# The time-step projection of a decoder block: four token sections side by side on four column groups of the matrix engine

## The chip, the cores and the metric

The kernel runs on one core of a Trainium2 chip. The time of a run is device time in microseconds; the kernel before was run three times (1519.18, 1522.98 and 1523.01 us), and its time is the median, 1522.98 us. One more execution was taken with the hardware profiler on. Profile and trace come from that one.

The engines that matter here: PE multiplies matrices (PEld is its loading of the stationary operand, which overlaps PE), DVE, ACT and POOL work on vectors, and SP only issues DMAs, in order. ACT issues some DMAs as well. DMAs of both run on the same 16 DMA engines.

## The reference

The reference is one decoder block for a batch of two sequences of 2048 tokens with 512 features: a Mamba-2 state-space mixer, a cross-attention over 77 context tokens, and a mixture of 16 expert slots, each added to its input and normalised. The change touches only the beginning of the mixer, the time step and its decay:

```python
proj = xs @ W_in.T
xBC, dt = (proj[..., :d_conv_c], proj[..., d_conv_c:])
...
dt = jax.nn.softplus(dt + dt_bias)
...
A = A_param * dt
cumA = jnp.cumsum(A, axis=1)
norm = (jnp.exp(cumA) * jnp.cumsum(jnp.exp(-cumA), axis=1))[..., None]
Y = ssd(xh, A, Bh, Ch, CHUNK)
out = Y[0] / norm
```

So for each token and each of 16 heads there is one number `dt`, the product of the token's 512 features with one column of `W_in`; it is summed along all 2048 tokens. Only the output of the scan of batch 0 is used (`Y[0]`), while the normaliser `norm` is taken of both batches.

## The kernel before

The work comes in stages. The first (lines 297 to 675, up to about 325 us of the span) has the in-projection, the convolution and the scan over 16 chunks of 128 tokens, for batch 0 alone, and beside them `decay` for batch 0 and for batch 1. The second mixes the tokens up to the second norm (up to about 950 us), then come the experts' weights, read from memory, and the combination of the slots.

`decay(b)` (line 373) works on a tile `z` of 128 rows by 512 columns. Its rows are four sections of 512 tokens, 32 rows each, of which 16 hold the heads; its columns are the tokens of a section. For each section `g` a tile `xs` with the section's tokens is loaded from `xT` (features on partitions, in four blocks `k` of 128) and multiplied with `wdt`, the 32 columns of the weight (16 of them zero), so that the result lands in the 32 rows of section `g` of a PSUM tile `dps`. For batch 0 `xs` holds all 512 tokens of a section (1 MB, in the buffers named "CS"); for batch 1 it holds 256 (512 KB, in the buffers named "sw"). Both have two buffers, which they share with others: "CS" with the scan's operand `CS` and one of the first weights, "sw" with the weights that `setup` loads. Then DVE adds the bias and copies the section's 32 rows to `z` (line 385), and the generator yields. After four sections, `decay` goes on with all of `z`: softplus, the sums along the tokens (`full_scan`, line 361), the weights `wtok` that the scan of batch 0 needs, and the normalisers `fd`, stored for the next stage.

All matmuls go through the helper `mm` (line 231 in the profile), copies through `cp` (line 234), the division of a number into a high and a low part through `split` (lines 234 and 242). The matmuls of `decay` are in float32, and such a matmul leaves two records in the trace; those of the projection, `pj`, are products of such high and low parts.

The order of the work is written down: `project`, `scan`, `decay`, `setup` and others are generators, and strings such as the one for the opening, `'PPPFFPPFPFPPPDDPPPPPDPPPPDDPPPPPSSSDSPSSSSS'`, say which of them takes the next step. D is a step of `decay(0)`; in the later strings V is one of `decay(1)`, U one of `setup`, S one of the scan and P one of the projection. A scheduler of the framework then orders the instructions of each engine's queue from that, by a simulation of its own. Each queue runs in its order.

In the first stage SP issues the loads of `xs`, the first weights, the stores of the projection's high and low parts (line 540), the loads of the scan's operands BS and CS from there (line 554, six for each chunk), the loads of `setup` (line 417), and the store of `fd` (line 410). The tokens for the projection (`xt`, line 321) are loaded by ACT's queue.

Of the kernel before, what the change touches and what calls it, by code (L numbers as in the profile page):

```python
# [8 lines left out]
FP = mybir.dt.float32  # L9
FR = mybir.dt.float32r  # L10
AF = mybir.ActivationFunctionType
ALU = mybir.AluOpType
# [13 lines left out]
# columns of the packed per-partition vectors  # L26
# [3 lines left out]
# columns of the packed shape constants  # L30
# [34 lines left out]
def merge(*flows):  # L65
    """Emit flows side by side, each given as (generator, steps), at the pace that ends them together."""
    todo = [[f, n, 0] for f, n in flows]
    while todo:
        f = min(todo, key=lambda t: t[2] / t[1])
        f[2] += 1  # L70
        try:
            next(f[0])
        except StopIteration:
            todo.remove(f)


def weave(flows, depth, lag):
    """Emit `depth` flows side by side; the next one starts `lag` steps after the last."""
# [145 lines left out]
def tile_decoder(ctx, tc, a, out, dbg=None, upto=9, opt=None):  # L224
# [68 lines left out]
    with ExitStack() as st:  # L293
        class Pools:
            """tiles by tag from pools of their own, so that the next phase takes over each pool's room as it falls free"""
# [33 lines left out]
        def first_operands():  # L329
            """the first tokens and the weights in the order of their use, in pieces"""  # L330
# [22 lines left out]
        # decay: dt, cumulative sums, normalisers in rows (section of 512 tokens, head)  # L353
# [19 lines left out]
        def decay(b):  # L373
            z, za, cum = (sb.tile([128, 512], FP, tag="dec", bufs=3, name=n) for n in ("z", "za", "cum"))
            for g in range(4):
                dps = ps.tile([128, 512], FP, tag="p", bufs=3, name="dps")
                gs = slice(32 * g, 32 * g + 32)
                w = 256 if b else 512
                for t in range(0, 512, w):
                    xs = sb.tile([128, 4, w], FP, tag="sw" if b else "CS", bufs=2, name="xs")  # L380
                    (nc.sync, nc.scalar)[EA.get("dq%d" % b, 0)].dma_start(
                        xs, a["xT"][b][:, g * 512 + t:g * 512 + t + w].rearrange("(k p) t -> p k t", p=128))
                    for k in range(4):
                        mm(dps[gs, t:t + w], wdt[:, k, :], xs[:, k, :], k == 0, k == 3)
                dve.tensor_scalar(z[gs, :], dps[gs, :], vec[gs, V_DTB:V_DTB + 1], None, ALU.add)
                yield
# [26 lines left out]
        def setup():  # L413
            """operands of the next phase from weights, a half at a time"""
# [5 lines left out]
            # cross-attention keys and values  # L420
# [32 lines left out]
            # dispatch queries folded with the key weights  # L453
# [91 lines left out]
        def scan_loads(c):  # L545
            """operands of one pass that holds the three hi/lo products of the 32 state rows"""
# [13 lines left out]
        def scan_ready(c):  # L560
            """token-major x (weighted) and B of a chunk"""
# [79 lines left out]
        def next_weights():  # L641
            """weights of the next phase, into the room that the in-projection's leave"""
# [8 lines left out]
        def spread(*flows):  # L651
            """names side by side, each given as (name, steps), at the pace that ends them together"""
            return "".join(n for _, _, n in sorted(((k + 1) / n, i, c) for i, (c, n) in enumerate(flows) for k in range(n)))
# [30 lines left out]
    def stats(pool_, z, p=128, tg=""):  # L684
        """mean and 1/std over the free axis of z [p, 512]; the latter from exp(-ln(var+eps)/2) and a Newton step"""
# [13 lines left out]
    with ExitStack() as st:  # L699
# [222 lines left out]
        # Two half periods of four quarters for every tile; a stage works on the tile `back` periods ago.  # L922
        # Each quarter holds one group of heads of the attention and one block of products.
# [5 lines left out]
        def period(p):  # L929
            """operations of one period, in the order of their issue"""  # L930
# [86 lines left out]
    if True:  # L1017
# [17 lines left out]
        # the combine's weights stay in the slabs 0, 1, 2: the keys' come before the last experts', the others after  # L1035
# [34 lines left out]
        # sums over the tokens, divided by the sums of the weights, with their features on the partitions  # L1070
# [20 lines left out]
        # the slots after the dispatch and their norm; feature 4p+j sits on partition p  # L1091
# [17 lines left out]
        def mean(v):  # L1109
            """mean over the features, on all partitions"""  # L1110
# [33 lines left out]
    if True:  # L1144
# [4 lines left out]
        def beat(e, at):  # L1149
            """scores of the tokens in the waits for the last expert's weights"""  # L1150
# [105 lines left out]
        # what the slots hold besides the experts' sums  # L1256
# [8 lines left out]
        def slots_now(on):  # L1265
            """the slots with what the experts gave so far"""
# [8 lines left out]
        def slot_heads(nm, on, PS, pool_, tags=("kr0", "kr1")):  # L1275
            """keys or values of the slots without their bias, features on the partitions"""
# [11 lines left out]
        def by_heads(dst, src, cv, n):  # L1288
            """block-diagonal over the heads of a group"""
# [25 lines left out]
        def early():  # L1315
            """the scores of all slots but the last experts': maxima, exponentials and their sums"""
# [44 lines left out]
    with ExitStack() as st:  # L1361
# [18 lines left out]
        def slot_outputs(b, m):  # L1380
            """values of the slots times the output weights for two groups of heads"""
# [4 lines left out]
        def split_outputs(b, m):  # L1386
            vp = vps.pop((b, m))
            if m == 0:
                # the weights of a head sum to one, so that its rows carry the output bias
# [203 lines left out]
```

## Time and profile before

| what | value |
|---|---|
| median of three runs | 1522.98 us |
| the runs | 1519.18 to 1523.01 us |
| span of the profiled execution, the only time given of it | 1526.7 us |
| PE busy | 1372.1 us, 90% |
| DVE busy | 905.6 us, 59% |
| ACT busy | 616.3 us, 40% |
| POOL busy | 446.2 us, 29% |
| `dps` matmuls | 96 records, 24.2 to 197.9 us |
| loads of `xs` | 12 DMAs, landing 4.1 to 10.9 us after issue |

A line of the chain of waits has a start, a length and what ran; "PE dps L231 x8" means eight records of matmuls that write `dps`. A line of the busy time by stretch has the stretch, its length, the busy time of PE, PEld, DVE, ACT and POOL, each with its number of instructions, then the granted clock of PE as a share of full speed, the share of time that the DMA engines were busy, and the GB/s that they moved. A row of a DMA view gives packets and bytes; a packet is one contiguous run. In a line of the waits, the engine and line on the left waited for what stands right of the arrow; then come the sum in us, the number of waits and the longest. Matmuls overlap, and the end of each is modelled, so a "busy" PE can hide short gaps.

### The profile page before, as it was taken

The numbers are of one execution on the slowest core, as the hardware profiler recorded it, in microseconds if no ns is written. First come the engines' busy times: TensorE is split into PE (matmuls) and PEld (weight loads), VectorE is DVE, ScalarE is ACT, GpSimd is POOL, SyncE is SP. The second block draws the span as 40 slices with busy tenths as digits, with TensorE's granted clock in tenths as the row PEclk, the third lists the DMA queues.
The fourth block names the chain that finished last, engine by engine and source line by source line (L and its number), as shares of the span: only waits on it lengthen the run. The fifth ranks groups of instructions, "written<-read, shape, count | busy, mean of one in ns | idle before, by whom it ended". The sixth has DMA issues, their size and how long they took to land.

```text
span 1526.7 us, 27382 instructions
## 1 busy us (share of the span) xinstructions
PE 1372.1 (90%) x10282; PEld 996.3 (65%) x10282; DVE 905.6 (59%) x2142; ACT 616.3 (40%) x1683; POOL 446.2 (29%) x496
## 2 busy tenths in 40 slices
PE   7899999978999999999999997948979788889896
PEld 5788889857888888888888875205544445433364
DVE  6897796856788888888888764001211111115597
ACT  5544443524565565665656552001000000104456
POOL 3644543535444444444443321000000000000054
PEclk9999998988999999999999998969989998999998
DMA  9797987895122221311110138898999999999447
GB/s 312 194 214 206 227 219 194 223 248 143 56 56 60 66 63 57 96 57 56 57 53 18 70 139 350 355 415 359 418 419 418 420 419 419 418 421 408 174 149 251
DMA packets 177499, 339.61 MB, mean 222 GB/s; under 512 B 12027, under 2 KB 123131, under 8 KB 152536
## 3 DMA queue, kind: packets, MB, share of 16 engines
q1 hardware_dynamic: 161072, 311.25, 58.5%
q10 hardware_dynamic: 16296, 26.62, 5.1%
q8 instruction: 81, 1.33, 0.4%
q14 instruction: 50, 0.41, 0.1%
HBM read 299.56 MB, written 38.27 MB: 221 GB/s over the span
## 4 chain that ended last, share of the span: by engine, by line
PE 60%; DVE 17%; DMA 15%; ACT 4%; issue 3%; SPq 1%; POOL 1%; ACTq 0%; POOLq 0%; DVEq 0%
PE mm L231 25%; DMA ew<-in_e_W 8%; PE pj L231 7%; PE up L231 7%; DMA ew<-in_e_Wg 5%; PE tr L826 3%; PE yac L231 2%; PE sc L231 2%; PE y L231 2%; PE dps L231 2%; PE uu L231 2%; PE gp L231 1%; DVE X L528 1%; ACT pp L816 1%; PE tr L719 1%
## 5 line engine op out<-in xcount | busy, mean ns | idle before, releaser
L231 PE MATMUL up<-ew,hT 128*32 128x512 f32 x944 | 134.7, 645 | 34.4 <-DMA ew<-in_e_W 30.9
L818 POOL TENSOR_TENSOR pp<-pp,den 128x308 f32<-128x308 f32 x128 | 90.1, 708 | 161.4 <-DVE den L817 109.0
L1174 ACT ACTIVATE sv<-up 128x512 f32<-128x512 f32 x32 | 19.1, 597 | 269.8 <-PE up L231 247.0
L1183 POOL MEMSET aT<- 128x512 f32 x16 | 8.3, 524 | 403.5 <-PE yac L231 401.8
L231 PE MATMUL mm<-xTh,cqh 128*128 128x256 f32 x256 | 76.2, 309 | 26.2 <-ACT xTh L234 26.2
L1233 DVE TENSOR_TENSOR Qc<-mm,vec 128x512 f32<-128x512 f32 x32 | 22.1, 691 | 125.3 <-PE mm L231 125.3
L242 DVE TENSOR_TENSOR xTl<-tr,xTh 128x512 fp32r<-128x512 f32 x32 | 21.3, 687 | 115.1 <-ACT xTh L234 115.0
L231 PEld LDWEIGHTS up<-ew,hT 128*32 128x32 f32 x944 | 26.0, 112 | 96.6 <-issue 56.7
L826 PE MATMUL tr<-cst,pp 128*77 128x128 f32 x512 | 80.6, 282 | 1.4 <-ACT pt L234 1.2
L231 PE MATMUL mm<-x1Th,w30h 128*128 128x256 f32 x256 | 76.9, 301 | 4.4 <-DVE ql L786 3.6
L816 ACT ACTIVATE pp<-sc,mx 128x77 f32<-128x77 f32 x240 | 75.4, 327 | 13.3 <-DVE mx L813 12.5
L234 ACT COPY pt<-tr 77x512 f32<-77x512 f32 x96 | 55.7, 582 | 61.2 <-PE tr L826 34.2
L231 PE MATMUL mm<-xTl,cqh 128*128 128x256 f32 x256 | 78.4, 308 | 1.2 <-DVE xTl L242 1.2
L231 PEld LDWEIGHTS mm<-xTh,cqh 128*128 128x128 f32 x256 | 51.5, 207 | 40.2 <-ACT xTh L234 30.2
L231 PE MATMUL mm<-xTh,cql 128*128 128x256 f32 x256 | 75.2, 296 | 0.0
L231 PE MATMUL mm<-x1Tl,w30h 128*128 128x256 f32 x256 | 74.4, 291 | 0.9 <-DVE x1Tl L722 0.9
L231 PE MATMUL mm<-x1Th,w30l 128*128 128x256 f32 x256 | 73.8, 288 | 0.0
L826 PEld LDWEIGHTS tr<-cst,pp 128*77 128x77 f32 x512 | 59.4, 148 | 16.3 <-issue 11.1
L234 ACT COPY raw<-pj 128x512 f32<-128x512 f32 x48 | 28.1, 584 | 99.1 <-PE pj L231 65.0
L231 PE MATMUL yac<-ew,aT 128*32 128x512 f32 x488 | 61.1, 637 | 7.1 <-issue 4.7
L744 POOL TENSOR_TENSOR ut<-ut,fb 128x512 f32<-128x512 f32 x32 | 41.0, 1282 | 80.4 <-DMA ut<-Ud 40.9
L231 PEld LDWEIGHTS mm<-xTl,cqh 128*128 128x128 f32 x256 | 52.3, 204 | 18.4 <-issue 14.7
(376 smaller groups left out, 4358.1 us busy)
## 6 DMA issues: line engine op xcount, KB each, us to landing
ew<-in_e_W SPq DMA_DIRECT2D x119, 1024.0 KB, 15.9
ew<-in_e_Wg SPq DMA_DIRECT2D x60, 1024.0 KB, 14.1
BS<-scrBc SPq DMA_DIRECT2D x48, 256.0 KB, 5.7
CS<-scrC SPq DMA_DIRECT2D x48, 256.0 KB, 6.2
xt<-in_x SPq DMA_DIRECT2D x32, 256.0 KB, 2.8
ut<-Ud SPq DMA_DIRECT2D x32, 256.0 KB, 3.4
fb<-fd SPq DMA_DIRECT2D x128, 64.0 KB, 3.0
x2d<-x ACTq DMA_DIRECT2D x32, 256.0 KB, 2.0
```

Of the source, the lines that this page charges most:

```text
L231: return pe.matmul(o, lhsT=l, rhs=r, start=start, stop=stop, **kw)
L234: (act.copy, dve.tensor_copy, pool.tensor_copy)[e](o, i)
L242: (lo_eng or dve).tensor_tensor(lo, src, hi, ALU.subtract)
L528: dve.scalar_tensor_tensor(dst, raw[:, j, 1 + t:1 + t + TB], w4[:, t:t + 1], dst, ALU.mult, ALU.add)
L719: pe.transpose(tp[:, k * 128:k * 128 + 128], src[:, k * 128:k * 128 + 128], ident)
L744: (act, dve, pool)[EN.get('uf', 1)].tensor_tensor(ut, ut, fb, ALU.mult)
L816: act.activation(pp[:, r, :], sv[:, r, :], AF.Exp, bias=mx[:, h:h + 1], accum_out=den[:, h:h + 1])
L818: (act, dve, pool)[EN.get('d%d' % hg, 2)].tensor_tensor(pp, pp, den[:, h4].unsqueeze(2).to_broadcast([128, 4, S]), ALU.mult)
L826: pe.transpose(tp[0:S, r * 128:r * 128 + 128], pp[:, r, :], ident)
L1174: last["silu"] = act.activation(sv, up, AF.Silu)
L1183: pool.memset(aT, 0.0)
L1233: dve.tensor_tensor(Qc[b][:, mp * 2:mp * 2 + 2, t1:t1 + TB], qq, vec[:, V_CQ + mp * 2:V_CQ + mp * 2 + 2].unsqueeze(2).to_broadcast([128, 2 ...
```

## The change

The loop over the four sections becomes a loop over four pieces of 128 columns. Each step of it makes 128 tokens of every one of the four sections: the `dps` tile is 128 by 128, with section `g` on rows 32g to 32g+31. The `xs` tile of a step holds, for each block `k`, the same 128 tokens of the four sections. For batch 0 one such tile holds all four blocks; for batch 1 a tile holds two blocks (`nk`), and a step uses two tiles; their sizes and buffers are those of before. Each block is loaded by a DMA of its own, 256 KB in runs of 128 tokens (512 bytes). The matmuls go over the blocks and, within a block, over the four sections, so that neighbours write different groups of 32 columns of the array. DVE then copies all 128 rows of a step at once, 128 columns wide. There are four steps and four yields for each batch, as before; the strings of the order are unchanged. Apart from this only comments were removed.

```diff
         def decay(b):
             z, za, cum = (sb.tile([128, 512], FP, tag="dec", bufs=3, name=n) for n in ("z", "za", "cum"))
-            for g in range(4):
-                dps = ps.tile([128, 512], FP, tag="p", bufs=3, name="dps")
-                gs = slice(32 * g, 32 * g + 32)
-                w = 256 if b else 512
-                for t in range(0, 512, w):
-                    xs = sb.tile([128, 4, w], FP, tag="sw" if b else "CS", bufs=2, name="xs")
-                    (nc.sync, nc.scalar)[EA.get("dq%d" % b, 0)].dma_start(
-                        xs, a["xT"][b][:, g * 512 + t:g * 512 + t + w].rearrange("(k p) t -> p k t", p=128))
-                    for k in range(4):
-                        mm(dps[gs, t:t + w], wdt[:, k, :], xs[:, k, :], k == 0, k == 3)
-                dve.tensor_scalar(z[gs, :], dps[gs, :], vec[gs, V_DTB:V_DTB + 1], None, ALU.add)
+
+            nk = 2 if b else 4
+            src = a["xT"][b].rearrange("(k p) (g t) -> p k g t", p=128, g=4)
+            for t in range(0, 512, 128):
+                dps = ps.tile([128, 128], FP, tag="p", bufs=3, name="dps")
+                for k0 in range(0, 4, nk):
+                    xs = sb.tile([128, nk, 4, 128], FP, tag="sw" if b else "CS", bufs=2, name="xs")
+                    for k in range(nk):
+                        (nc.sync, nc.scalar)[EA.get("dq%d" % b, 0)].dma_start(xs[:, k], src[:, k0 + k, :, t:t + 128])
+                    for k in range(nk):
+                        for g in range(4):
+                            mm(dps[32 * g:32 * g + 32, :], wdt[:, k0 + k, :], xs[:, k, g, :], k0 + k == 0, k0 + k == 3)
+                dve.tensor_scalar(z[:, t:t + 128], dps, vec[:, V_DTB:V_DTB + 1], None, ALU.add)
                 yield
```

## The prediction

> **What bounds the kernel now.** I read the page's busy table and slices first, to see which engines are full in the first fifth of the span, where both calls of `decay` run; then the busy time by stretch, the chain of waits, and the rows of single groups.
>
> ```profile
> span 1526.7 us, 27382 instructions
> PE   7899999978999999999999997948979788889896
> DVE  6897796856788888888888764001211111115597
> DMA  9797987895122221311110138898999999999447
> ```
> Slices are 38.2 us. In the first eight (in-projection and scan) PE, DVE and the DMA engines are all near full: whatever is taken from one can be caught by another.
>
> ```profile
> 24.20:53.30 29.10, 29.10 (x154) 17.37 (x153) 20.54 (x32) 15.07 (x28) 17.14 (x19) 1.00 0.94 265
> 53.30:95.00 41.70, 36.31 (x329) 33.24 (x333) 41.49 (x61) 19.64 (x38) 19.46 (x21) 1.00 0.67 163
> 95.00:110.00 15.00, 15.00 (x154) 13.29 (x154) 15.00 (x22) 9.37 (x19) 10.45 (x10) 1.00 1.00 265
> 110.00:200.00 90.00, 88.36 (x766) 74.13 (x765) 71.05 (x129) 39.48 (x75) 41.79 (x53) 1.00 0.84 213
> ```
> Columns: stretch, length, busy PE, PEld, DVE, ACT, POOL, granted clock, DMA share, GB/s. From 24 to 53 us (decay of batch 0) PE is full and DVE has 8.6 us idle. From 53 to 110 DVE is full. From 110 to 200 (decay of batch 1) PE is full again and DVE has 19 us idle.
>
> ```profile
> 24.27 0.98 PE dps L231 x2
> ...
> 26.82 2.69 PE dps L231 x6
> ...
> 31.88 3.55 PE dps L231 x8
> ...
> 41.76 3.55 PE dps L231 x8
> ...
> 49.72 3.56 PE dps L231 x8
> ...
> 53.31 0.77 DVE z L385
> ...
> 112.78 6.44 DMA xs<-in_xT
> ...
> 145.35 3.57 PE dps L231 x16
> ```
> This is the chain that ended last (start, us, what). All four sections of batch 0 are on it, and it hands over to DVE at 53.3. A matmul in float32 leaves two records, so x8 is four matmuls of 512 columns and x16 eight of 256. Batch 0 takes 0.98+2.69+3.55+3.55+3.56 = 14.3 us of the chain; the pieces of batch 1 (1.76, 1.62, 0.17, 3.57, 3.45, 1.84, 1.84) sum to 14.3. Together **28.6 us**.
>
> **The change part by part.**
>
> *Matmuls.* Before: 16 of 512 columns, 32 of 256, one column group at a time. After: 4 steps per batch, each with 16 matmuls of 128 columns, neighbours on different column groups. The trace has such work:
>
> ```profile
> 959.75 1.03 PE L231 MATMUL up<-ew,hT 128*32 128x512 f32 x8
> 960.61 1.03 PE L231 MATMUL up<-bb,cst 128*32 128x512 f32 x8
> 487.48 0.36 PE y L231 x8
> 490.36 0.79 PE y L231 x24
> ```
> `up` starts its next eight records after 0.86 us; one `dps` section, the same eight records on one group, took 3.55. So four groups really run at once. One new step is 32 records: by `up` cut to a quarter of the columns, 4 x 0.215 = 0.86 us; by `y` (128 columns, 24 in a row) 32 x 0.79/24 = 1.05; by a lone eight, with its change of shape on both sides, 4 x 0.36 = 1.44. I take 1.1, nearest the long run of `y`. Eight steps cost 8.8 us (6.9 to 11.5), so PE gives back 28.6 - 8.8 = **19.8 us**, 9.9 for each batch.
>
> *Evictions.* Before, eight of 32x512 at 746 ns = 6.0 us of DVE. After, eight of 128x128. The nearest row from PSUM is `kst`, 128x154, 371 ns; a copy of one column takes 149. I take 0.33: 2.6 us, and DVE gives back 3.3 us (3.0 to 4.8). The step's wait shrinks too: DVE sat 11.1 us before the `z` of L385 for `dps`, 7.4 of it in batch 0, with the convolution's instructions queued behind.
>
> *How much passes on.* Batch 0: PE reaches the end of its last section 9.9 us earlier, and DVE must do 20.5 us less 1.7 of work in a stretch of 19.2; it can just do it, if its idle time goes to nothing. Of the 8.6 us idle 7.4 was the wait for `dps`, which mostly goes; what is late next is the wait for ACT's convolution copies (1.4). Upper end 9.9, lower end 1.7 (DVE's own saving alone, if its full stretch after 53 absorbs the rest); I take 7, near the upper end because the idle time was named. Batch 1: the first step lies around 111-121 where DVE has just been full, the other three where PE never idles and DVE has 19 us of room. Ends 9.9 and 1.6; I take 7. **-14 us**.
>
> *The loads.* Twelve DMAs (four of 1 MB, eight of 512 KB) become 32 of 256 KB, and their contiguous runs go from 2 KB and 1 KB to 512 B. All are issued on SP. The 20 more cost 20 x 0.39 = 7.8 us of SP's time; SP otherwise waits (47.3 us for `gp` alone), and nothing computes on it. What stands behind them on SP: the stores of the hi and lo parts, then the BS and CS loads, which land a median 5.7 and 6.2 us after issue, and today no `gp` waits for them. Against that, an xs buffer is now held for 1.1 us of PE instead of 3.6, so SP's 16.7 us of waiting for `dps` at the xs issues shrinks. The transfer itself:
>
> ```profile
> DMA packets 2588, 3.66 MB, mean 366 GB/s; under 512 B 633, under 2 KB 1212, under 8 KB 2588
> ...
> DMA packets 1542, 0.77 MB, mean 192 GB/s; under 512 B 46, under 2 KB 1542, under 8 KB 1542
> ```
> The first is 10 to 20 us (xs and weights, mostly 2 KB and longer), the second 84 to 88 us (BS and CS, 512 B), both with all 16 engines busy. 4.19 MB at 366 GB/s is 11.5 us, at 192 it is 21.8: up to 10.4 us more of DMA time per batch. BS and CS write 32 partitions at a time and xs all 128, so the truth may lie lower. In batch 0 half of it falls where the engines are already 0.94 busy: the second, third and fourth steps may each find their piece 1 to 3 us late; by my times they want it at about 28, 35 and 41 us, and it can be issued at 18, 29 and 32. In batch 1 the share is 0.84 and 14 us are free. Ends: a gain of 0.8 (the one wait of PE for xs goes, since pieces land one by one) and a loss of 10.4; I take a loss of 1.5, nearer the first, since the earlier buffer release starts the loads sooner.
>
> The Trainium skill, "DMA: Bandwidth & Descriptors", gives 512 B as the least transfer for line rate (Specifications); the 192 GB/s row does not agree. By that rule the load term would be 0 and the sum -14.0. The same page's rule in Bandwidth, to batch DMAs to 1 MiB and more, speaks against this change; its fit of 2.0 us plus bytes by 436 GB/s would, as an estimate for pieces in series, make each megabyte 4 x 2.6 = 10.4 us instead of 4.4, some 48 us over eight megabytes, and the change slower. The 366 GB/s above, with 512 KB and 1 MB loads in flight together, shows that loads here do not run in series.
>
> *Order.* The scheduler that orders each engine's queue may place things differently. The nearest row is the first section, split into x2 and x6 with 1.6 us of `pj` between: plus or minus 1.6 for each batch, taken as 0.
>
> **Sum:** -14 + 1.5 = -12.5 us on the profiled span of 1526.7, the only time shown of that execution. It lies 0.2% above the median of the runs, 1522.98, to which I apply the difference: **1510.5 us**, own range 1504 to 1517. No change can be told from one within 0.3%, or 4.6 us.
>
> **Rivals.**
> 1. *All of PE's saving passes on*: DVE keeps up and the loads stay hidden. 1523.0 - 19.8 = 1503. For it: PE is on the chain through both stretches, without one wait for DVE in the first. Against: DVE would need to be 98% busy.
> 2. *DVE takes over*: the stretch from 53 on is DVE's, so an early PE only waits; the gain is DVE's own 3.3 us, 1519.7 (1517 to 1522). For it: 41.49 of 41.70. Against: DVE's idle time before it was spent waiting for `dps`.
> 3. *SP's queue holds the loads (slower).* This row, of the queue waits in the first 5 us, is an issue held by an earlier, unrelated load:
> ```profile
> SPq L339 <- DMA xt<-in_xT: 2.2, 1, 2.2
> ```
> Six weight loads took 7.17 us to issue so, 1.2 each. If each of the 20 more xs issues is held like that, batch 0 has 12 x 1.2 = 14.4 us more in the queue, and the last section ends about 4 us later than now, not 9.9 earlier; batch 1 has 9.6 more ahead of the CS loads against the 7 gained, +2.6. 1523 + 6.6 = 1529.6. It decides from about 14/20 = 0.7 us of hold an issue. Against: later issues, with fewer loads in flight, took 0.3 to 0.5 us.
>
> **How the numbers follow.** Forecast 0.50, rival 1 0.18, rival 2 0.19, rival 3 0.13. Faster: 0.50 + 0.18 + the better 0.08 of rival 2 = 0.76; same: its other 0.11 and 0.01 of rival 3, 0.12; slower 0.12. The range runs from 1502 (the lower third of rival 1, 0.06, left out) to 1525 (rival 3 left out): all but 0.19.
>
> **What would show it.** Right: `dps` pieces of about 1.1 us on the chain, 9 us in all; `z` eight times at about 0.33 us; the hand-over to DVE near 43 to 46 us, the scan's end some 12 us earlier. The load term shows as PE idle before `dps` for xs, or `gp` for CS. Wrong if `dps` steps stretch while waiting for pieces, if DVE after 45 us is full and the gain at 110 us is under 3 us, or if SP waits on landings at the xs issues grow by more than 10 us.

## The result and the profile after

The changed kernel takes **1512.64 us** (median of six runs, 1504.8 to 1516.61). The kernel before, run beside it, takes 1522.99 us. The ratio is 0.9928, with a 95% interval of 0.9902 to 0.9955: 10 to 11 us faster. A second set of runs of the same two kernels gave 0.992 (0.9892 to 0.9949). The forecast was 1510.5.

The two profiled executions differ by much more: spans 1526.7 and 1502.8, 23.9 us apart. That isn't the size of the effect. The profiled execution of the changed kernel is the fastest of its six, and the one of before lies above its median. Repeated profiles of the same programs (before again: span 1522.8, after again: 1508.6) agree with the first ones to 1.5 us up to 340 us, while the rest of the span differs by 3 and 7 us. So I read the effect at a place in the first fifth, called here the first product of the second stage: the first `tr` (line 719, after the change 721). It stands behind 36 records of that stage's output products, which are the first to use what the scan stored.

The trace's times (us) at six places; "again" is a second profile of the same program.

| place | before | before again | after | after again |
|---|---|---|---|---|
| last `z` copy of batch 0 ends | 54.1 | 53.7 | 48.7 | 48.2 |
| `wtok` copied | 70.6 | 70.3 | 69.8 | 69.4 |
| scan's second store | 128.5 | 127.9 | 126.5 | 127.0 |
| last `z` copy of batch 1 ends | 199.1 | 198.5 | 192.6 | 193.1 |
| scan's last store | 325.9 | 324.5 | 315.3 | 314.2 |
| **first product of the second stage** | **338.0** | **337.2** | **327.2** | **325.8** |
| span | 1526.7 | 1522.8 | 1502.8 | 1508.6 |

The lead is 10.7 us (after again: 12.2) where the first stage ends, which is what the timed runs show. In the second stage PE's queue is nearly the same in both kernels (all but 12 of some 4400 instructions stand in the same order), so I don't put the other 13.2 us of the spans' difference down to the change.

The chain of waits of the changed kernel, from 33 us on (start, us, what):

```profile
33.11 1.40 DVE X L530 x2
...
35.84 4.57 DVE X L530 x6
...
42.94 0.26 DVE z L387
43.20 3.79 DVE Bc L530 x7
...
48.42 0.27 DVE z L387
...
56.11 3.25 DVE C L530 x3
...
64.39 5.01 DVE X L530 x2
...
69.91 0.61 DVE wtok L401
...
70.56 1.11 PE gp L231 x4
```
The four `dps` sections that stood on the chain between 24 and 53 us are gone from it. In their place stand convolution instructions of DVE, up to the copy of `wtok`. The chain then passes to PE.

The groups of the changed step (count, busy us, mean ns, idle before), of before and then of after:

```profile
L231 PE MATMUL dps<-xs,wdt 128*32 128x256 f32 x64 | 14.9, 381 | 0.8 <-DMA xs<-in_xT 0.8
L231 PE MATMUL dps<-xs,wdt 128*32 128x512 f32 x32 | 14.7, 596 | 0.0
...
L385 DVE TENSOR_SCALAR z<-dps,vec 32x512 f32<-32x512 f32 x8 | 6.0, 746 | 11.1 <-PE dps L231 11.1
```
```profile
L231 PE MATMUL dps<-xs,wdt 128*32 128x128 f32 x256 | 11.7, 284 | 0.0
...
L387 DVE TENSOR_SCALAR z<-dps,vec 128x128 f32<-128x128 f32 x8 | 2.7, 341 | 2.1 <-PE dps L231 2.1
```
PE has no wait before `dps` in this profile, and DVE's wait for it fell from 11.1 to 2.1 us.

Busy time by stretch (columns as before: PE, PEld, DVE, ACT, POOL, granted clock, DMA share, GB/s):

```profile
24.20:45.00 20.80, 20.80 (x242) 17.71 (x244) 20.63 (x26) 10.87 (x21) 17.15 (x19) 1.00 1.14 312
45.00:90.00 45.00, 39.14 (x338) 35.32 (x330) 41.93 (x64) 20.66 (x40) 19.25 (x20) 0.92 0.78 178
90.00:105.00 15.00, 14.62 (x156) 12.95 (x156) 14.95 (x25) 10.21 (x20) 8.40 (x12) 1.00 1.02 240
105.00:190.00 85.00, 80.98 (x807) 72.72 (x806) 73.39 (x123) 40.34 (x78) 44.54 (x53) 0.96 0.90 227
```
DVE has 0.17 us idle of 20.8 in the first stretch, where it had 8.6 of 29.1. New against before, up to 190 us, is the clock below 1.00 (before has such stretches later). One stretch of 5 us shows it, of before and then of after:

```profile
70.00:75.00 5.00, 4.24 (x37) 4.00 (x36) 4.96 (x10) 3.92 (x9) 1.07 (x2) 1.00 0.23 77
```
```profile
70.00:75.00 5.00, 4.44 (x20) 4.38 (x21) 4.74 (x7) 1.98 (x4) 2.59 (x4) 0.55 0.31 105
```
PE is about as busy in both, but at 0.55 it gets 20 matmuls through instead of 37. The timeline of after shows what came just ahead (in brackets the idle time before an instruction, and its releaser):

```profile
70.56 1.11 PE L231 MATMUL gp<-CS,BS 96*128 96x128 f32 x4 [2.36 <-DVE wtok L401]
...
108.58 1.11 PE L231 MATMUL gp<-CS,BS 96*128 96x128 f32 x4 [2.39 <-DVE kst L434]
```
PE, further ahead than before, stands twice for a copy that DVE has in its queue behind the convolution; at full clock four such records take 0.66 us (at 77.86 us).

**An account of the stage.** For all that follows I take PE's busy time from 24 us to the second stage's first product, of all its work and of `dps` alone. Before:

```profile
24.00:338.00 314.00, 297.52 (x2478) 248.77 (x2477) 252.79 (x414) 140.45 (x267) 148.24 (x164) 0.96 0.85 217
24.00:338.00 314.00, 29.58 (x96) 0.96 0.85 217
```
After:
```profile
24.00:327.20 303.20, 283.34 (x2638) 248.78 (x2637) 258.76 (x414) 139.91 (x266) 149.74 (x165) 0.95 0.90 226
24.00:327.20 303.20, 11.32 (x254) 0.95 0.90 226
```
The stretch is `dps`, PE's other matmuls, and PE idle: 29.6 + 267.9 + 16.5 = 314.0 before, 11.3 + 272.0 + 19.9 = 303.2 after. So PE gave back 18.3 us, of which 4.1 went into the same other matmuls at a lower clock and 3.4 into idle time, and 10.8 came through. The repeated profiles, set against each other, share it out otherwise: 17.9 given back, 0.5 into other matmuls, 6.0 into idle time, 11.4 through. So the idle time is in both, and the clock's share is not settled. The same account for every run, with the times at which the fourth and the fifth of the scan's eight stores start:

| run | `dps` | PE's other matmuls | PE idle | 4th store | 5th store | first product of the second stage | ratio of times |
|---|---|---|---|---|---|---|---|
| before | 29.6 | 267.9 | 16.5 | 203.0 | 239.7 | 338.0 | |
| before again | 29.5 | 268.7 | 15.1 | 202.4 | 239.1 | 337.2 | 0.9997 |
| after | 11.3 | 272.0 | 19.9 | 199.0 | 230.7 | 327.2 | 0.9928 |
| after again | 11.5 | 269.1 | 21.1 | 199.4 | 229.9 | 325.8 | 0.992 |
| loads cut | 29.4 | 264.7 | 15.9 | 204.8 | 238.5 | 333.9 | 0.9991 |
| quarter of the matmuls | 8.5 | 267.2 | 17.5 | 189.3 | 222.6 | 317.3 | 0.9898 |
| quarter, and loads cut | 7.9 | 270.2 | 21.6 | 195.1 | 228.3 | 323.7 | 0.9923 |
| section by section | 23.9 | 270.1 | 17.1 | 203.8 | 235.8 | 335.1 | 0.9942 |
| batch 0 only | 22.2 | 270.3 | 18.3 | 206.0 | 239.1 | 334.7 | 0.9959 |
| after, copies on ACT | 11.3 | 269.0 | 18.9 | 196.3 | 226.7 | 323.2 | 0.9921 |
| before, copies on ACT | 28.5 | 263.7 | 14.4 | 201.3 | 234.6 | 330.6 | 0.9962 |
| block by block | 10.2 | 270.9 | 23.7 | 199.9 | 231.9 | 328.8 | 0.9941 |
| before, less GpSimd | 29.1 | 265.2 | 12.6 | 203.6 | 232.2 | 331.0 | 0.992 |
| after, less GpSimd | 12.5 | 272.6 | 17.0 | 197.1 | 227.4 | 326.0 | 0.9892 |

The two stores show when the lead arises. No `dps` matmul and no `z` copy runs between them, in any kernel. Before and its repeat need 36.7 us from one to the other, every other run 28.6 to 33.7, also where `dps` takes as long as in before (loads cut: 33.7). The lead of the changed kernel is 4.0 us at the fourth store and 9.0 at the fifth (repeat against repeat: 3.0 and 9.2). Before and then after:

```profile
203.00:240.00 37.00, 35.08 (x286) 30.19 (x285) 31.67 (x48) 16.13 (x32) 15.14 (x17) 0.91 0.84 210
```
```profile
203.00:240.00 37.00, 37.00 (x310) 32.53 (x307) 28.57 (x50) 17.03 (x33) 15.94 (x22) 0.95 0.82 221
```
Here PE of before stands idle for 1.9 us and has the lower clock. So 3 us or more of each run's lead arise where nothing changed runs, and no run shows why every order of the queues but that of before does better there.

### The profile page after: what moved, and what is told of

The parts are those of the page before. It is cut to its first block, busy times and chain, and to the rows that moved or that the text cites. A ratio compares the mean times of both kernels' runs of the same rounds, so it can differ in the third digit from the quotient of the medians.

```text
span 1502.8 us, 27725 instructions
## 1 busy us (share of the span) xinstructions
PE 1348.9 (90%) x10442; PEld 992.5 (66%) x10442; DVE 910.4 (61%) x2142; ACT 616.5 (41%) x1683; POOL 447.6 (30%) x496
## 4 chain that ended last, share of the span: by engine, by line
PE 58%; DVE 17%; DMA 17%; ACT 4%; issue 3%; POOL 1%; SPq 1%; ACTq 0%; POOLq 0%; DVEq 0%
PE mm L231 27%; DMA ew<-in_e_W 9%; PE up L231 6%; DMA ew<-in_e_Wg 6%; PE pj L231 5%; PE tr L828 4%; DVE X L530 3%; PE sc L231 3%; PE y L231 2%; PE yac L231 2%; PE gp L231 1%; PE uu L231 1%; DVE C L530 1%; PE tr L721 1%; DMA ut<-Ud 1%
## 5 line engine op out<-in xcount | busy, mean ns | idle before, releaser
L1176 ACT ACTIVATE sv<-up 128x512 f32<-128x512 f32 x32 | 19.1, 597 | 270.2 <-PE up L231 260.5
L818 ACT ACTIVATE pp<-sc,mx 128x77 f32<-128x77 f32 x240 | 75.4, 327 | 11.1 <-DVE mx L815 10.3
L828 PEld LDWEIGHTS tr<-cst,pp 128*77 128x77 f32 x512 | 59.8, 148 | 16.7 <-issue 10.3
L530 DVE SCALAR_TENSOR_TENSOR X<-raw,vec,X 128x256 f32<-128x256 f32 x80 | 66.4, 876 | 5.4 <-ACT X L526 4.9
## 6 DMA issues: line engine op xcount, KB each, us to landing
ew<-in_e_W SPq DMA_DIRECT2D x119, 1024.0 KB, 15.9
```

The costliest lines, as they stand in the source:

```text
L530: dve.scalar_tensor_tensor(dst, raw[:, j, 1 + t:1 + t + TB], w4[:, t:t + 1], dst, ALU.mult, ALU.add)
L818: act.activation(pp[:, r, :], sv[:, r, :], AF.Exp, bias=mx[:, h:h + 1], accum_out=den[:, h:h + 1])
L828: pe.transpose(tp[0:S, r * 128:r * 128 + 128], pp[:, r, :], ident)
L1176: last["silu"] = act.activation(sv, up, AF.Silu)
```

## The experiments

The first runs are the kernel before again, the loads alone, the matmuls alone, and the change without its alternating column groups.

**Before, again.** The program of before, unchanged.

> The kernel before, once more, for a second profile of it: which part of the 24 us between the two profiles lies outside the stage that was changed, and comes and goes between executions. The first profile of before spans 1526.7 us, that of after 1502.8, while the medians differ by 10.3. If the stages behind the scan vary from execution to execution, this profile has its first stage as the first one had it (first product of the second stage near 338 us, within 2) and the rest shorter, span 1515 to 1525. If the change itself made the later stages shorter, the second stage takes 585 us again, as in the first profile, and not the 576 of after.

1524.81 us, ratio 0.9997 (0.9975 to 1.0019). The second stage's first product comes 0.7 us earlier than in the first profile and the end 3.9 us earlier. This is the noise that the other readings have to pass.

**The loads alone.** Before, with its twelve loads cut into 32 of 256 KB in runs of 512 bytes, as the change has them.

```diff
-                    (nc.sync, nc.scalar)[EA.get("dq%d" % b, 0)].dma_start(
-                        xs, a["xT"][b][:, g * 512 + t:g * 512 + t + w].rearrange("(k p) t -> p k t", p=128))
+                    for u in range(0, w, 128):
+                        (nc.sync, nc.scalar)[EA.get("dq%d" % b, 0)].dma_start(
+                            xs[:, :, u:u + 128], a["xT"][b][:, g * 512 + t + u:g * 512 + t + u + 128].rearrange("(k p) t -> p k t", p=128))
```

> The kernel before, its matmuls and evictions untouched, but each load of xs cut into DMAs of 128 tokens: 32 of 256 KB in runs of 512 bytes, as many as in the change. The theory (the loads cost 1.5 us beside the gain) expects 1524 to 1526 against 1523, no difference that can be told. The rival that the smaller loads cost as much as 512-byte rows moved at 192 GB/s expects up to 10 us for batch 0 where the DMA engines are busy, 1530 to 1535. The rival that SP is held at each issue expects 1529 or more, with CS loads late and PE waiting for them.

1522.85 us, ratio 0.9991 (0.9974 to 1.0008): no difference. The issues, in the view of the tile `xs` (duration min/median/max in ns, first and last start):

```profile
L382 SPq DMA_DIRECT2D xs<-in_xT x32: 367/504/1463, 11.0 to 191.7; - x32
```
They take SP's time (504 ns at the median, against 389 for the loads of before), PE waits 1.0 us for `xs` in all, and PE's long sections cover it. So the third rival (SP's queue) and the price of many small DMAs fall for this place: beside 28.6 us of matmuls, 32 loads cost what 12 did. The first product comes 4.1 us earlier than in before all the same; up to the fourth store this run is 1.8 us behind, so that a few us at that place can come with another order of the queues alone.

**A quarter of the matmuls.** Before, with only the first of the four feature blocks multiplied; the other three are left out of the time step. PE's time on `dps` falls to 8.5 us, a little below the change's, with the old loads and evictions.

```diff
-                    for k in range(4):
-                        mm(dps[gs, t:t + w], wdt[:, k, :], xs[:, k, :], k == 0, k == 3)
+                    mm(dps[gs, t:t + w], wdt[:, 0, :], xs[:, 0, :], True, True)
```

> The kernel before with only the first of the four feature blocks multiplied; the time step is then not the reference's: three quarters of its products are left out. Loads, evictions and order of the steps are as before, so that PE has some 21 us less on these matmuls, a little more than the 18.3 that the change gave back, and nothing else is changed. If PE's time is what pays and the loads take 1.5 us, this gains 13 to 17 us: 1506 to 1510. If DVE takes over as soon as PE is shortened, 3 us at most beyond what the change gained is out of reach and it stays at 1513 to 1520. If the change's gain came from the smaller evictions or the earlier loads and not from PE, this is at 1520 to 1523.

1509.57 us, ratio 0.9898 (0.9877 to 0.9919). The account of this run, all of PE's work and `dps` alone:

```profile
24.00:317.30 293.30, 275.77 (x2402) 240.32 (x2401) 257.94 (x413) 140.32 (x267) 151.92 (x162) 0.96 0.91 231
24.00:317.30 293.30, 8.53 (x24) 0.96 0.91 231
```
`dps` gives back 21.1 us and the first product comes 20.7 us earlier, as much as if all of it passed on; at the fourth store, behind the last `dps`, the lead is 13.7. DVE, which has even the slow evictions of before here, does not stop it. PE's longest wait of this run:

```profile
PE op L231 <- DVE cum L362: 4.9, 1, 4.9
```
One wait of 4.9 us for DVE, with a clock of 0.86 in the 25 us around it, does not undo the gain.

**The sections one after another.** After, with the same loads, tiles and evictions, but the matmuls of a section issued together, so that neighbours write the same column group.

```diff
-                    for k in range(nk):
-                        for g in range(4):
-                            mm(dps[32 * g:32 * g + 32, :], wdt[:, k0 + k, :], xs[:, k, g, :], k0 + k == 0, k0 + k == 3)
+                    held.append(xs)
+                for g in range(4):
+                    for k in range(4):
+                        mm(dps[32 * g:32 * g + 32, :], wdt[:, k, :], held[k // nk][:, k % nk, g, :], k == 0, k == 3)
```

> The kernel after, same tiles, loads and evictions, but the sixteen matmuls of a step in another order: all four blocks of one section, then the next section, so that neighbours write the same column group and can't run at once. If the column groups are what gave PE its time back, the matmuls of the step take 2.5 to 3.5 us instead of 1.1, some 12 to 18 us more of PE in all, and most of the gain is lost: 1519 to 1526. If the gain lay in the loads, the evictions or the other order of the queues, the time stays at 1511 to 1514.

1516.13 us, ratio 0.9942 (0.9922 to 0.9963). The last step of batch 0 in the timeline:

```profile
49.22 2.46 PE L231 MATMUL dps<-xs,wdt 128*32 128x128 f32 x32
```
The same 32 records take 1.01 us to the next matmul in the changed kernel and 2.39 here: it is the alternation of the column groups that makes the step short, a factor of 2.4, and not the smaller pieces. At the second stage's first product the lead shrinks to 2.9 us. The time does not follow: I had expected most of the gain to go (1519 to 1526 us), and by the medians this kernel keeps 8 of the change's 10 to 11 us; the intervals overlap. Its `dps` is still 5.7 us shorter than before's, and it has the change's evictions. So the run shows what the alternation does to `dps`, not how much of the kernel's time hangs on it.

The next question was why 7 us of PE's 18.3 don't come through. The first theory was the two waits for DVE's copies with the low clock behind them.

**After, again.** The changed program as it is.

> The kernel after, once more, for a second profile. In the first, PE waited twice for DVE, 2.4 us before a score product at 70.6 us (for wtok) and 2.4 us before one at 108.6 us (for kst), and behind both the granted clock was at about half for some 6 us. If the order of the queues makes these waits, both are there again within 1 us, the clock falls again, and the second stage begins near 327 us. If the clock falls by chance, this profile has it elsewhere or not at all, and that start moves by several us. What lies behind the first stage should differ by up to 8 us from the first profile, as the two profiles of before differ by 4.

1511.07 us (1507.87 to 1512.43), ratio 0.992 (0.9892 to 0.9949); the same two waits of 2.4 us. A low clock is behind them again, but for a shorter time behind the first: 0.78 and 0.88 in the two stretches of 5 us from 70 us, where the first profile had 0.55 and 0.77.

**The two copies on ACT, after and before.** `wtok` and `kst` are copied out of PSUM by ACT, not DVE.

```diff
-                dve.tensor_copy(wtok, wp)
+                act.copy(wtok, wp)
...
-                    dve.tensor_scalar(kst[:, m, :], kp[:, 0:B * S], vec[:, V_KB + m:V_KB + m + 1], RS, ALU.add, ALU.mult)
+                    act.activation(kst[:, m, :], kp[:, 0:B * S], AF.Identity, bias=kbr[:, m:m + 1], scale=RS)
```

> The kernel after, with the two copies out of PSUM that PE waited for (wtok and kst) made by ACT instead of DVE; a small tile of scaled biases is added for it. The theory: of the 18.3 us that PE got back, some 8 are lost because PE, now ahead of DVE, stands in its queue for these two copies and then runs at half clock. Then this removes 2 x (2.4 + about 3) = 8 to 11 us, and the second stage begins near 318 us, time 1501 to 1506. The rival, that the smaller loads are what is lost, or that DVE is simply full, expects no more than DVE's own 2 us: 1510 to 1513.

1510.85 us, ratio 0.9921 (0.9893 to 0.9948), the same as the change without it. Both waits are gone, and others stand in their place:

```profile
PE pj L231 <- ACT raw L234: 3.6, 3, 1.9
PE dps L231 <- DMA xs<-in_xT: 2.0, 2, 1.4
```

> The kernel before with the same two copies moved to ACT. PE waited there for these two 0.8 and 0.9 us, at full clock. The theory expects 1 to 3 us of gain, 1520 to 1523; if the move is worth 8 us here too, it is an improvement of its own and says nothing on the change.

1517.02 us, ratio 0.9962 (0.9947 to 0.9976), the first product 7.4 us earlier: the same edit helps the kernel before. In the changed one its 2.6 to 4.0 us at that place (323.2 against 327.2 and 325.8) do not show in the time. The theory, which expected 1501 to 1506 us, falls. The two copies were a cost of their own in before, and in the changed kernel their removal only shows the next waits.

**Batch 0 block by block.** After, but batch 0 goes over the four feature blocks with one load of 1 MB each (runs of 8 KB), four column groups of 512 columns, and a single eviction. Batch 1 is as in the change.

```diff
+                dps = ps.tile([128, 512], FP, tag="p", bufs=3, name="dps")
+                for k in range(4):
+                    xs = sb.tile([128, 4, 512], FP, tag="CS", bufs=2, name="xs")
+                    nc.sync.dma_start(xs.rearrange("p g t -> p (g t)"), a["xT"][b][k * 128:k * 128 + 128, :])
+                    for g in range(4):
+                        mm(dps[32 * g:32 * g + 32, :], wdt[:, k, :], xs[:, g, :], k == 0, k == 3)
+                    if k == 3:
+                        dve.tensor_scalar(z, dps, vec[:, V_DTB:V_DTB + 1], None, ALU.add)
```

> The kernel after, but batch 0 goes over the four feature blocks instead of the four pieces of tokens: each step loads one block of all 2048 tokens by one DMA of 1 MB in runs of 8 KB and multiplies 512 columns of each section on its column group; one PSUM tile takes all four steps and is copied out once. PE's work is that of the change (about 0.9 us a step), DVE's evictions for batch 0 are one of about 0.7 us instead of four of 0.34, the DMAs four instead of sixteen. If the pieces of 512 bytes cost something in the opening, where the DMA engines are busy all the time, this gains 2 to 8 us on the change: 1505 to 1510. If the loads are hidden there, 1510 to 1514.

1513.38 us, ratio 0.9941 (0.9918 to 0.9963): no better than the change. `dps` is as short (10.2 us) and the loads are few, but nothing of `z` is there before the last block has landed, `wtok` comes at 74.1 us instead of 69.8, and PE is idle 23.7 us, most of all runs.

**A quarter of the matmuls and the loads cut.** The two edits to before at once; three of the four feature blocks are again left out of the time step.

```diff
+                    for u in range(0, w, 128):
+                        (nc.sync, nc.scalar)[EA.get("dq%d" % b, 0)].dma_start(
+                            xs[:, :, u:u + 128], a["xT"][b][:, g * 512 + t + u:g * 512 + t + u + 128].rearrange("(k p) t -> p k t", p=128))
+                    mm(dps[gs, t:t + w], wdt[:, 0, :], xs[:, 0, :], True, True)
```

> The kernel before, with the time step multiplied over the first of its four feature blocks only (the other three are left out, so TensorE's time falls as much as with column groups or more) and its tokens fetched by 32 loads of 512-byte runs. The same cut of the products with the old loads put the second stage's first product 20.6 us earlier (317.3 us) and the time at 0.990 of before; the change, with the small loads and about the same TensorE time, put it 10.7 and 12.2 us earlier (327.2 and 325.8 us). Theory A (the small loads are harmless; what separates the two is the order of the matmuls and the evictions): the second stage's first product within 3 us of 318 us, the time 1508 to 1512 us, ratio 0.989 to 0.993. Theory B (once TensorE is short, the small loads hold back what stands behind them on SP's queue): near 325 to 328 us, the time 1512 to 1517 us, ratio 0.993 to 0.996.

1512.15 us, ratio 0.9923 (0.9901 to 0.9944). The first product comes at 323.7 us, 6.4 us later than with the old loads; it lies between the two theories, nearer to the one in which the loads cost. The time takes the other side: 0.9923 lies in the range of theory A. By the account the 6.4 are 2.9 of other matmuls and 4.1 of idle, less 0.6 of `dps`: the same two terms in which the change loses its 7 in its first profile. SP's queue of the quartered kernel with the old loads (start, us, what; each row a stretch of issues):

```profile
17.12 8.14 SPq L381 DMA_DIRECT2D xs<-in_xT  x2
25.45 1.44 SPq L539 DMA_DIRECT2D scrBc<-hi  x1
...
32.58 1.67 SPq L553 DMA_DIRECT2D BS<-scrBc  x3
```
And with the loads cut:
```profile
19.39 11.28 SPq L382 DMA_DIRECT2D xs<-in_xT  x10
30.77 1.31 SPq L540 DMA_DIRECT2D scrBc<-hi  x1
...
37.04 6.48 SPq L554 DMA_DIRECT2D BS<-scrBc  x4
```
The first store of the high part leaves 5.3 us later and the first BS load 4.5 us later, behind ten `xs` issues on SP; by the copy of `wtok` the kernel is 5.4 us behind (71.8 against 66.4) and stays so. That the one makes the other isn't shown: no engine is seen to wait for these stores or BS loads. Two other waits for landings stand ahead of `wtok` in this run and not in the one with the old loads:

```profile
PE dps L231 <- DMA xs<-in_xT: 1.8, 1, 1.8
```
```profile
ACT xh L234 <- DMA xt<-in_xT: 4.1, 1, 4.1
```
In the changed kernel the same two issues leave at 28.1 and 36.2 us. The timed ratios (0.9898 and 0.9923) point the same way, but their intervals overlap. The framework's scheduler also gave another order (2312 of PE's 2498 instructions of the stage stand in the same order), so that this prices the loads together with the order that came with them.

**Batch 0 alone.** After for batch 0, before for batch 1.

```diff
+            if b == 0:
+                for t in range(0, 512, 128):
...
+                        for k in range(nk):
+                            for g in range(4):
+                                mm(dps[32 * g:32 * g + 32, :], wdt[:, k0 + k, :], xs[:, k, g, :], k0 + k == 0, k0 + k == 3)
...
+            else:
+                for g in range(4):
...
+                        for k in range(4):
+                            mm(dps[gs, t:t + w], wdt[:, k, :], xs[:, k, :], k == 0, k == 3)
```

> The change for batch 0 alone; batch 1, which runs from about 145 to 200 us, stays as before. Theory A (each batch passes on its own part, as the prediction's sum has it, 7 us a batch): the second stage's first product 5 to 7 us earlier than before (331 to 333 us) and a time of 1516 to 1519 us, ratio 0.995 to 0.998; by 110 us the stage stands as in the changed kernel, some 6 us ahead. Theory B (batch 0's lead is lost by 130 us to VectorE and GpSimd, so that all that lasts comes from batch 1): the first product within 3 us of before's 338.0, ratio 0.998 to 1.001. Theory C (batch 0 gives it all): 326 to 328 us, ratio 0.991 to 0.994.

1518.49 us, ratio 0.9959 (0.9944 to 0.9975). The time fits theory A; the trace fits it less. `dps` of batch 0 falls from 14.3 to 5.4 us, `z` is done 5.7 us earlier, the scan's second store comes 2.6 us *later* than before, and the first product 3.2 us earlier. At the fourth store it is still 3.0 us later than before, so that all of the 3.2 arises behind that store, where before is slow. This is where the lead of batch 0 goes:

```profile
70.00:95.00 25.00, 23.39 (x193) 20.10 (x194) 19.86 (x32) 6.66 (x14) 3.18 (x5) 0.80 0.60 131
```
PE is 94% busy in these 25 us at a clock of 0.80 and gets 193 matmuls done, against 223 at 1.00 in before; it stands 2.4 us for `wtok` ahead of them. By the difference to the whole change batch 1 passes on 7.5 (after again: 8.9) of its 9 us.

**Less work on GpSimd, before and after.** Left out of both kernels: the low part of the projection's tokens after block 0 (that of block 0 is used again) and the low parts of the convolved rows (the high parts are stored twice).

```diff
-            split(xh, xl, xt, engs[EA.get("xl", 2)], EA.get("xh", 0))
+            cp(EA.get("xh", 0), xh, xt)
...
-                    split(hi, lo, cv[nm], engs[EA.get("cl", 2)], EA.get("ch", 0))
+                    cp(EA.get("ch", 0), hi, cv[nm])
```

> The kernel before without two of GpSimd's kinds of subtraction in the first stage (left out: the low part of the projection's tokens after block 0, where that of block 0 is used again, and the low parts of the convolved rows, where the high parts are stored twice): 23 of its 70 elementwise products and 58 of their 126 us go, nothing else. Theory A (a convolution instruction on VectorE stands while GpSimd has the tiles' port, 1354 ns beside a GpSimd product against 476 alone, 47.6 us in all): those 47.6 us fall to about half, 20 to 30 us, but TensorE bounds much of this stage, so that the second stage's first product comes 5 to 15 us earlier. Theory B (the long convolution instructions are long for another reason): their excess stays over 40 us and the first product within 3 us of before's 338.

1513.56 us, ratio 0.992 (0.9899 to 0.9941), first product at 331.0, 7.0 us earlier than in before.

> The changed kernel without the same two kinds of GpSimd's subtractions as in the run before this one (the same parts left out). Theory A (after the change VectorE is the bound and 6 to 7 us of the gain go into its waits beside GpSimd): against the kernel before with the same cut, the second stage's first product comes 15 to 19 us earlier, most of the 18.3 us that TensorE got back, and the time is 15 to 18 us shorter than that kernel's. Theory B (the part that isn't passed on is lost elsewhere: the scan's dependences, the clock behind TensorE's waits): the two still stand 9 to 13 us apart, as the changed kernel and the kernel before do.

1507.63 us, ratio 0.9892 (0.987 to 0.9914), first product at 326.0: only 5.0 us ahead of its partner, and 5.9 us by the medians, less than either theory has. The theory under test was that the changed kernel loses its gain to DVE's waits beside GpSimd, where a convolution instruction takes 1354 to 1470 ns on average instead of 476. That excess summed to 47.6 us of the stage in before, 54.9 after; here it is 15.0 and 13.0. The mechanism is real and the theory falls all the same: with most of the excess gone the changed kernel gains little over itself at that place (326.0 against 327.2 and 325.8; 3 to 5 us by the medians, with overlapping intervals), and the two kernels lie closer together, not further apart. Part of the reason stands in the timeline of the changed kernel with less GpSimd:

```profile
112.08 1.21 PE L231 MATMUL dps<-xs,wdt 128*32 128x128 f32 x16 [4.74 <-DMA xs<-in_xT]
```
and in its stretches:
```profile
110.00:115.00 5.00, 2.92 (x36) 1.93 (x36) 1.59 (x6) 0.00 (x0) 0.61 (x1) 0.51 0.42 140
115.00:120.00 5.00, 5.00 (x30) 4.72 (x23) 4.14 (x8) 0.71 (x1) 1.69 (x2) 0.50 0.56 126
```
Now PE does stand for a load of `xs`, 6.1 us in three waits, with half the clock behind it. One caution: with the high part stored twice, its buffer is held by the stores, and DVE waits 7.5 us (5.8 in the partner) for them before the next copy into it.

**What is settled and what isn't.** That less time of PE on these matmuls shortens the kernel is shown in the time by the quarter of the matmuls; that the alternating column groups make `dps` short is shown step by step by the sections one after another. How much of the change's 10 to 11 us hangs on the alternation is not shown, since that run keeps 8 of them, and neither is why 3 us or more of each lead arise between the fourth and the fifth store. That what fails to come through is PE idle is read off the account in both profiles; the lower clock is plain in one of them. No single wait carries it: each one that I took away (two copies, GpSimd's collisions, the small loads of batch 0) was followed by another. The quartered kernel gains as much as its PE gets back, with the same work for DVE, so DVE's work alone doesn't set the limit. Cut loads, with the order that came with them, took 6.4 us from it, which is the size of what is missing, but a changed kernel with few loads and otherwise its own steps was not run, and block by block, which has few loads for batch 0, gained nothing. So the loads' share in the changed kernel stays open between 0 and about 6 us.

## Why the prediction was right, and where it wasn't

*Matmuls.* Predicted 8.8 us of `dps`, bounds 6.9 to 11.5; measured from start to next start 10.3 (again: 10.6). A step of 32 records in one piece takes 1.01 us, as `y` said. But the scheduler set twelve eights alone between other work, at 0.35 to 0.36 us most of them, which is the price of the upper bound. PE gave back 18.3 instead of 19.8.

*Evictions.* Predicted 0.33 us each, measured 341 ns; 6.0 us became 2.7, the forecast 3.3 us saved. Right.

*How much passes on.* Predicted 7 of each batch's 9.9. The sum held, the split did not: batch 0 alone brought 3.2 us at the end of the stage (and was 3.0 us behind at the fourth store), batch 1 by difference 7.5 to 8.9. The step that failed is the reading of batch 0, in which I named DVE's idle time but not what comes after it: DVE did fill its 8.6 us, its queue then held `wtok` and `kst` back, and PE paid for that in the wait (2.4 us, in both profiles) and in the clock behind it (0.55 and 0.77 in the next 10 us, in the repeat 0.78 and 0.88). The prediction had no term for the clock. Its own warning, DVE full after 45 us and under 3 us of gain at 110, nearly came true: DVE is busy 41.93 of 45 us, and the scan's second store, at 126.5 us, leads by 2 us.

*The loads.* Predicted +1.5 through pieces that land late. In the changed kernel PE waited for `xs` not at all in the first profile and 0.5 us in the second, and beside long matmuls the cut loads cost nothing (0.9991). Beside short matmuls they put the end of the stage 6.4 us later in the quartered kernel. How they did so is open: PE waited 1.8 us for a piece there, as the prediction had it, and ACT 4.1 us for the projection's tokens, while the stores and BS loads left SP some 5 us later. The prediction had weighed that queue (7.8 us of SP's time) and called it free because SP otherwise waits; no engine's wait in the trace says otherwise. If the quartered kernel stands for the changed one, the term is mis-sized, and the term of what passes on is too small by about as much. The two errors would then cancel in the sum: 18.3 - 6.4 = 11.9 us, against the forecast 12.5 and the measured 10.7 and 12.2. No run shows that they do. The estimate of some 48 us more, which the prediction set aside, comes from a fit that its page gives for DMAs issued from GpSimd, while these are issued by SP; the run with the cut loads shows nothing of it.

*Order.* The scheduler did reorder PE's queue (2222 of before's 2571 instructions of the stage stand in the same order). The runs don't price that by itself.

*The signs named ahead.* The last `dps` step of batch 0 ends at 45.3 us, in the range named for the hand-over; DVE holds the chain already from 33 us. The scan's last store comes 10.6 and 11.7 us earlier, against "some 12".

*The sum.* -12.5 us forecast; -11.0 and -12.2 by the two ratios. Part of this agreement is luck. Behind the last changed step, at the fourth store, only 4.0 us (repeat against repeat: 3.0) of the lead are there; 5 to 6 us more arise up to the fifth, in a stretch that the prediction doesn't speak of and where before is slower than every other run. The first rival (1503) falls in the times, although the single profiled run of 1504.8 looks like it. In the quartered kernel as much as PE's saving did pass on, though only 13.7 of the 21 us were there at the fourth store. The second (DVE takes over, 1519.7) is half right for batch 0 and wrong for the whole. The third (SP's queue, slower) falls: an `xs` issue of the changed kernel took 676 ns at the median, 0.3 us more than the 389 of before, where it decides from 0.7. Seven in a row took 10.5 us of SP, not enough to turn the sign.

## What to carry to other kernels

Alternating small stationary operands over the four column groups shortens such float32 matmuls by a factor of about 2.4 against the same pieces section by section, and PE's saving is worth having where PE stands on the chain. What an engine gives back is not lost or kept as a whole: account the stage as the step, the engine's other work and its idle time, since the rest can come back as idle time or as a slower clock on instructions that nobody touched. And judge the effect from several runs and at several places, not from two spans: here 13 of 24 us between the two profiles arose in later stages whose instructions hadn't changed, and about half of the lead at the stage's end arose in a stretch where nothing changed runs.

## What the hardware showed that I had not expected

- Behind a gap of 2.36 us on PE the granted clock was 0.55 and 0.77 in the two stretches of 5 us from 70 us on, and `gp` took 1.11 us instead of 0.66; behind the same gap in the repeat it was 0.78 and 0.88. The Trainium skill, "TensorE: Matmul & The Clock Gate" (What's actually happening), has the clock fall after an idle window of about 3.4 us; here less stood ahead of it. In before a gap of 2.81 us, at 66 to 69 us, left the clock at 1.00 in the stretches around it, while one of 1.4 us, up to 226 us, stood ahead of 0.79 and 0.53 in the two stretches of 5 us from 225 us on. So the length of one gap doesn't decide it.
- A convolution instruction of DVE takes 476 ns alone and on average 1354 to 1470 ns when a GpSimd subtraction or product runs beside it, up to 2.6 us, about the length of a GpSimd subtraction (2.5 us). With 58 us of GpSimd's subtractions taken away the largest group fell so, changed kernel first, then the one with less GpSimd:

```profile
L530 DVE SCALAR_TENSOR_TENSOR X<-raw,vec,X 128x256 f32<-128x256 f32 x80 | 66.4, 876 | 5.4 <-ACT X L526 4.9
```
```profile
L529 DVE SCALAR_TENSOR_TENSOR X<-raw,vec,X 128x256 f32<-128x256 f32 x80 | 42.8, 578 | 6.8 <-ACT X L525 6.5
```
  The Trainium skill, "SBUF — State Buffer" (SBUF: two separate sides), describes such a lock, one side standing until the other's instruction is over; the longest of these durations agree with that.
